# A four-layer graph network on one core: the due times of its planned instruction order are set anew

## The chip, the cores and the metric

The kernel runs on one core of a Trainium2 chip. The core has five engines that matter here: TensorE (PE; matmuls, with PEld for its weight loads), VectorE (DVE), ScalarE (ACT), GpSimd (POOL) and SyncE (SP), which issues all the kernel's DMAs from one queue. The metric is the device time of one execution in microseconds (us); the time before is the median of three runs.

## The reference

128 graphs of 64 nodes carry 512 features in float32. Four layers follow each other, each on a normalized and rectified copy of x, and each added to x:

```python
for each layer: h = max(layernorm(x), 0); x = x + layer(h, adj)
layer 0: relu(conv(h, W1)), layernorm with gamma and beta, conv(., W2), + h
         conv(h, W) = Dn * H @ (Be * H^T @ (h @ W^T)) + b,   H = (adj != 0)
layer 1: s = (h @ w) @ a;  A = exp(leaky(8 tanh((s_i + s_j) / 8))) * adj, rows normalized
         and scaled by the row sums of adj;  A @ h @ w
layer 2: exp(q k^T) * adj, rows normalized, @ v   with q, k, v = h @ Wq, Wk, Wv + biases
layer 3: transition = rows of adj * exp(leaky(s_i + s_j + ab)), normalized
         relu(sum over k = 0..2 of transition^k @ h @ Wk[k] + bk[k])
```

## The kernel before

The rows (128 graphs x 64 nodes) are cut into 16 groups of four tiles of 128 rows, two graphs to a tile. Layers 0 and 1 run over all 16 groups first, with W1, W2 and w resident; x after layer 1 goes to DRAM (xm). Then layers 2 and 3 run over the 16 groups, in the same memory with other tiles: the product Wq^T Wk (made at the start, L477, kept in DRAM as wg_d) and Wv take W1's place (wa_mem), and layer 3's weights are streamed for every group from seven prepared factors in DRAM (fac), which GpSimd works out beside layers 0 and 1 (setup_w3).

All the larger products are in a form with seven block products in place of eight: `strassen` (L691, layers 0 and 1), `prod` in layer2 (L930, called lq for the logits' side and v for the values) and `product` in layer3 (L1124, both by blocks and nested, so 7 x 7 small products of three 128x128 matmuls for k). VectorE makes the sums and differences of the operands (L683, L916, L1091, L1104), ScalarE and VectorE take the results out of PSUM. Transposes go through ScalarE (L601, L603) and a transposing DMA (L602). Layer 3's weights land in three buffers wf (L1116), two loads for each of the seven products, 768 and 576 KB; in the last group two other buffers serve as well. PSUM has eight buffers (ps), shared by everything.

The order of the work is not the order of the code. Each operation is recorded with an engine, an estimated cost and a due time (`Graph.op`); `Graph.run` then plays the whole program once with these costs, before anything is emitted, and emits the instructions in the order that results. At each step it looks, for every engine, at the operations whose inputs are ready and whose buffers are free, takes those that can start soonest, and among them the one with the smallest due time. Each engine then works through its own list strictly in that order on the chip. Where the plan leaves TensorE idle for more than 1 us and a PSUM buffer is free, `fill` puts matmuls on a tile of ones (L1199), so many that half the foreseen gap is filled.

A due time is `G.prio + G.shift`. `G.prio` begins at the group's number times PERIOD1 (layers 0 and 1) or, behind 16 times PERIOD1, times PERIOD2 (layers 2 and 3), and grows within a layer by the cost of each TensorE step times that layer's STRETCH. `G.shift` is the offset from the table AT that `part(name)` sets for the part of the program being recorded: g0 to g3 and g (the product Wq^T Wk and its way to DRAM), bq (a bias from Wk), x0, w1, w2, w (first loads), l0, l1, l3 (preparations), c1, c2, c (sums of weight blocks), wg (load and sums of layer 2's weights), m to y1 (layer 0), s to e1 (layer 1), hT to pv (layer 2), s3 to b0 (layer 3), ws (layer 3's weight loads), load1 to load3. beg0 and beg1 are added to `G.prio` for the first group, end00, end01 and end11 in layers 0 and 1 of the last two groups, new2 and new3 for the first, end2 and end3 for the last group of layers 2 and 3.

```python
pick = min(((t, o) for t, o in can if t <= by), key=lambda c: (c[1].prio, c[1].seq))
```

Of the kernel before, what the change touches and what calls it, by code (L numbers as in the profile page):

```python
# [171 lines left out]
def tile_adj_preln_d4(  # L172
# [40 lines left out]
    def size(shape):  # L213
        n = 1
        for d in shape[1:]:
            n *= d
        return n

    for two in TWO:
        both = work.tile([P, max(sum(size(shape) * n for _, shape, n in tags) for tags in two)], F32,  # L220
                         name="_".join(tag for tags in two for tag, _, _ in tags))
        for tags in two:
            at = 0
            for tag, shape, n in tags:
                for i in range(n):
                    v = both[:, at:at + size(shape)]
                    at += size(shape)
                    if len(shape) == 3:
                        v = v.rearrange("p (a b) -> p a b", a=shape[1])
                    elif len(shape) == 4:  # L230
                        v = v.rearrange("p (a b c) -> p a b c", a=shape[1], b=shape[2])
# [52 lines left out]
    def quad(b):  # L284
# [2 lines left out]
    FILL, LAT = 0.5, 2.3  # L287


    STRETCH, PERIOD1, PERIOD2 = (2.4612, 8.078, 75.6572, 3.3564), 83.325, 154.352  # L290
    AT = {
        "x0": -994.6, "apart": -498.0, "w1": 324.19, "b1": 226.55, "w2": 2150.56, "w": 142.04, "c1": -38.37, "l0":
        -925.08, "c2": 112.02, "l1": -0.36, "c": -1301.28, "g0": -738.7, "g1": -448.93, "g2": -273.36, "g3":
        -517.97, "g": -716.27, "bq": -558.39, "l3": -245.42, "wg": -1135.2, "wp": 1053.37, "beg0": -576.12, "beg1":
        -46.39, "end00": 344.71, "end01": 1612.85, "end11": 614.38, "new2": -75.28, "new3": -60.89, "end2": -113.22,
        "end3": -536.67, "load1": -428.24, "load2": 720.79, "m": -35.26, "h0": -17.03, "p0": 19.05, "z0": -475.95,
        "q0": 27.48, "y0": -539.17, "h1": -22.94, "p1": -22.85, "z1": -30.23, "q1": 5.26, "y1": -136.9, "s":
        -548.75, "t0": -653.3, "e0": -587.74, "t1": -339.5, "e1": -183.15, "hT": 477.73, "sh": -540.0, "lq": 571.58,
        "pt": 1630.65, "v": -264.99, "pv": 1213.51, "s3": 1112.96, "tt": 524.31, "a0": 1110.99, "b0": -1096.16,
        "a1": 1142.82, "ws": 1188.92, "load3": -885.85, "bk": 940.93,  # L300
    }

    def part(name):
# [997 lines left out]
def _program(arrays, n_tokens):  # L1301
    import concourse.bacc as bacc

    nc = bacc.Bacc("TRN2", target_bir_lowering=False, num_devices=1)
    args = [nc.dram_tensor(f"in_{k}_dram", arrays[f"in_{k}_dram"].shape, F32, kind="ExternalInput").ap()
            for k in _NAMES]
    args.append(nc.dram_tensor("out_0_dram", (n_tokens, D), F32, kind="ExternalOutput").ap())
    with tile.TileContext(nc) as tc:
        tile_adj_preln_d4(tc, *args)
    return nc  # L1310
# [12 lines left out]
```

## Time and profile before

| | us |
|---|---|
| median of 3 runs (2337.66 to 2342.29) | 2342.09 |
| the profiled execution, its own time | 2345.87 |
| its span, first to last instruction | 2344.1 |
| TensorE busy | 2292.1 |
| VectorE busy | 1859.1 |
| ScalarE busy | 1388.6 |
| GpSimd busy | 1201.2 |

The profile gives times in us unless marked ns. "Busy" is the union of an engine's instructions; 14280 matmuls are among the 39830 instructions. In answers by windows the columns are: the window, its length, the busy time and count of PE, PEld, DVE, ACT and POOL, then the granted TensorE clock (1 is full), the busy share of the 16 DMA engines, and GB/s. Lists in order of time give start, length, engine, line, operation, output and inputs, and in brackets the idle time before and what ended it. L691 is line 691 of the kernel.

The 16 DMA engines are busy a third of the time in layers 0 and 1 and nearly four fifths in layers 2 and 3, where they move some 220 GB/s. The kernel moves 355 MB in all.

### The profile page before, as it was taken

The page shows a single profiled execution, that of the slowest core. Times are in us where ns is not written, and L with a number is a line of the kernel's source. Part 1 is how long each engine was busy: PE and PEld are TensorE (multiplying, and loading weights), DVE is VectorE, ACT ScalarE, POOL GpSimd, SP SyncE. Part 2 cuts the span into 40 slices and gives each one's busy share as a digit, 9 for nine tenths or more (in the row PEclk, how much of TensorE's full clock was granted, in tenths as well). Part 3 has the DMA queues.
Part 4 walks back from the last instruction along what each step waited for, and adds up shares of the span by engine and source line. Part 5 has one row for each costly group of instructions (what it writes and reads, how often), then busy time and mean ns, then how long its engine had stood idle before and what let it go on. Part 6 is the DMA issues. An engine that isn't in the chain of part 4 may idle for free.

```text
span 2344.1 us, 39830 instructions
## 1 busy us (share of the span) xinstructions
PE 2292.1 (98%) x14280; PEld 1873.0 (80%) x14280; DVE 1859.1 (79%) x4004; ACT 1388.6 (59%) x1993; POOL 1201.2 (51%) x1771
## 2 busy tenths in 40 slices
PE   8999999999999999999999999999999999999997
PEld 4576677776777767777688899999899999999997
DVE  7887887887878777777857778878788888788886
ACT  4666565575555666556746566556566656656642
POOL 7345556545565455554323455445555545555533
PEclk9999999999999999999999999999999999999999
DMA  7343333333333432323415877777787787797757
GB/s 247 85 99 88 78 91 80 96 91 79 79 89 94 96 74 67 78 64 81 106 57 148 237 215 231 216 225 216 219 229 224 222 222 220 211 245 226 224 180 229
DMA packets 403478, 355.12 MB, mean 151 GB/s; under 512 B 290896, under 2 KB 321872, under 8 KB 403280
## 3 DMA queue, kind: packets, MB, share of 16 engines
q1 hardware_dynamic: 403280, 352.58, 54.8%
q8 instruction: 112, 1.84, 0.3%
q14 instruction: 86, 0.70, 0.1%
HBM read 241.05 MB, written 44.33 MB: 122 GB/s over the span
## 4 chain that ended last, share of the span: by engine, by line
PE 79%; DMA 6%; DVE 4%; ACT 3%; issue 1%; POOL 1%; SPq 0%; DVEq 0%; ACTq 0%; POOLq 0%
PE ps L691 34%; PE ps L1124 18%; PE ps L930 15%; PE ps L592 4%; DMA w2m_wm_a_wf<-fac 3%; PE ps L844 2%; PE ps L1067 2%; PE ps L999 2%; PE ps L961 1%; DMA adj<-in_adj_dram 1%; DMA rw<-row 1%; ACT h L583 1%; DMA h<-o 1%; ACT o L601 1%; DVE st L562 1%
## 5 line engine op out<-in xcount | busy, mean ns | idle before, releaser
L583 ACT ACTIVATE h<-x,nm,rs 128x512 f32<-128x512 f32 x384 | 308.6, 816 | 251.3 <-POOL nm L570 233.9
L564 POOL TENSOR_SCALAR rs<-mv 128x1 f32<-128x1 f32 x320 | 118.3, 371 | 388.0 <-DVE mv L563 362.1
L1124 PE MATMUL ps<-w2m_wm_a_wf 128*128 128x128 f32 x2256 | 295.7, 276 | 5.1 <-DMA w2m_wm_a_wf<-fac 4.5
L1124 PEld LDWEIGHTS ps<-w2m_wm_a_wf 128*128 128x128 f32 x2256 | 277.1, 193 | 10.3 <-issue 2.9
L691 PE MATMUL ps<-w2m_wm_a_wf,s_s_zz 128*128 128x256 f32 x1152 | 276.9, 379 | 4.5 <-DVE s_s_zz L683 4.0
L1124 PE MATMUL ps<-w2m_wm_a_wf,tmp_mB_xi 128*128 128x128 f32 x1968 | 259.0, 277 | 10.1 <-DMA w2m_wm_a_wf<-fac 6.6
L691 PEld LDWEIGHTS ps<-w2m_wm_a_wf,s_s_zz 128*128 128x128 f32 x1152 | 217.1, 190 | 52.4 <-issue 18.9
L1124 PEld LDWEIGHTS ps<-w2m_wm_a_wf,tmp_mB_xi 128*128 128x128 f32 x1968 | 239.4, 193 | 15.3 <-issue 4.9
L691 PE MATMUL ps<-w2m_wm_a_wf,rT_vu_tt 128*128 128x256 f32 x1024 | 240.0, 381 | 4.1 <-ACT u L659 2.4
L691 PE MATMUL ps<-wa_mem,mT_sx 128*128 128x512 f32 x512 | 239.1, 593 | 0.8 <-DMA wa_mem<-in_W1T_dram 0.5
L691 PEld LDWEIGHTS ps<-w2m_wm_a_wf,rT_vu_tt 128*128 128x128 f32 x1024 | 193.7, 191 | 42.9 <-issue 11.3
L565 POOL TENSOR_TENSOR rs<-rs,mhalf 128x1 f32<-128x1 f32 x320 | 208.6, 652 | 25.3
L562 DVE BATCH_NORM_STATS2 st<-x 128x6 f32<-128x512 f32 x256 | 175.4, 685 | 15.3 <-DMA x<-xm 7.7
L691 PE MATMUL ps<-wa_mem,s_s_zz 128*128 128x512 f32 x384 | 181.1, 595 | 1.4 <-DVE z_hT L711 1.4
L691 PEld LDWEIGHTS ps<-wa_mem,mT_sx 128*128 128x128 f32 x512 | 96.0, 190 | 106.5 <-issue 98.8
L570 POOL TENSOR_SCALAR nm<-mv,rs 128x1 f32<-128x1 f32 x320 | 159.3, 498 | 31.2
L603 ACT COPY rT_vu_tt<-z_hT 128x1024 uint16<-128x1024 uint16 x128 | 146.6, 1159 | 18.1 <-DMA z_hT<-tmp_mB_xi 17.9
L601 ACT COPY o<-h 128x1024 uint16<-128x1024 uint16 x128 | 134.0, 1048 | 32.5 <-DVE h L1056 29.5
L592 PEld LDWEIGHTS ps<-bd,h 128*128 128x128 f32 x1024 | 127.4, 192 | 25.7 <-DVE bd L873 10.5
L831 ACT ACTIVATE z_hT<-z_hT,nm,rs 128x512 f32<-128x512 f32 x128 | 103.6, 811 | 66.7 <-POOL nm L570 66.5
L982 POOL TENSOR_TENSOR u<-u,wp_bv_bk 128x512 f32<-128x512 f32 x48 | 61.4, 1280 | 155.9 <-ACT u L634 155.9
L601 ACT COPY tmp_mB_xi<-z_hT 128x1024 uint16<-128x1024 uint16 x128 | 133.7, 1045 | 9.3 <-issue 3.0
(205 smaller groups left out, 4975.8 us busy)
## 6 DMA issues: line engine op xcount, KB each, us to landing
w2m_wm_a_wf<-fac SPq DMA_DIRECT2D x110, 768.0 KB, 5.2
w2m_wm_a_wf<-fac SPq DMA_DIRECT2D x109, 576.0 KB, 4.8
x<-xm SPq DMA_DIRECT2D x128, 256.0 KB, 3.8
x<-in_x_dram SPq DMA_DIRECT2D x64, 256.0 KB, 2.8
xm<-x SPq DMA_DIRECT2D x64, 256.0 KB, 2.0
out_dram<-x SPq DMA_DIRECT2D x64, 256.0 KB, 3.7
adj<-in_adj_dram SPq DMA_DIRECT2D x32, 256.0 KB, 3.4
fac<-wp_bv_bk SPq DMA_DIRECT2D x63, 128.0 KB, 2.0
```

Of the source, the lines that this page charges most:

```text
L562: dve(0.69, lambda i=i: nc.vector.bn_stats(st.t[:, i, :], src(i)), [r[i]], [(st, i)])
L564: small(0.28, lambda: nc.gpsimd.tensor_scalar_add(rs.t, mv.t[:, 1:2], EPS), [mv], [rs])
L565: small(0.62, lambda: nc.gpsimd.tensor_tensor(rs.t, rs.t, mhalf, ALU.pow), [rs], [rs])
L570: small(0.32, lambda: nc.gpsimd.tensor_scalar(nm.t, mv.t[:, 0:1], rs.t, -1.0, op0=ALU.mult, op1=ALU.mult), [mv, rs], [nm])
L583: act(0.82, lambda: nc.scalar.activation(h.t, xx.t, AF.Relu, bias=nm.t, scale=rs.t), [xx, nm, rs], [h])
L592: nc.tensor.matmul(quad(p)[:, c, :], h.t[:, c * P:(c + 1) * P], rhs(), start=True, stop=True)
L601: act(1.05, lambda: nc.scalar.copy(u16(planes.t).rearrange("p (q c) -> p q c", q=2), u16(src()).rearrange("p (c q) -> p q c", q=2)), ksrc, ...
L603: act(1.16, lambda: nc.scalar.copy(u16(dst()).rearrange("p c (k q) -> p c k q", q=2), u16(back()).rearrange("p (q c r) -> p c r q", q=2, c ...
L691: nc.tensor.matmul(p.t[:, :n], lhs()[:, c, :], rhs(c), start=first and c == 0, stop=c == kc - 1, skip_group_check=True)
L831: act(0.72, lambda half=half, rs=rs, nm=nm: nc.scalar.activation(half(), half(), AF.Identity, bias=nm.t, scale=rs.t), [(z, j), rs, nm], [( ...
L930: nc.tensor.matmul(pair(p.t)[:, o, :], a, b, start=first and o == 0 and c == 0, stop=c == 1, skip_group_check=True)
L1124: nc.tensor.matmul(inner(p, q)[:, r, :], at()[:, k, :], wv()[:, r, k, :], start=first and r == 0 and k == 0, stop=k == 2, skip_group_check ...
```

## The change

Only numbers change: the four stretches, the two periods and the 61 offsets of AT. No operation, cost, buffer or dependency is touched. The new numbers come from a choice that judges an order by its planned time and by two replays of it, with transfers landing later and with work taking longer.

```diff
-    STRETCH, PERIOD1, PERIOD2 = (2.4612, 8.078, 75.6572, 3.3564), 83.325, 154.352
+    STRETCH, PERIOD1, PERIOD2 = (2.4948, 23.7591, 14.6346, 4.8494), 85.831, 149.366
     AT = {
-        "x0": -994.6, "apart": -498.0, "w1": 324.19, "b1": 226.55, "w2": 2150.56, "w": 142.04, "c1": -38.37, "l0":
-        -925.08, "c2": 112.02, "l1": -0.36, "c": -1301.28, "g0": -738.7, "g1": -448.93, "g2": -273.36, "g3":
-        -517.97, "g": -716.27, "bq": -558.39, "l3": -245.42, "wg": -1135.2, "wp": 1053.37, "beg0": -576.12, "beg1":
-        -46.39, "end00": 344.71, "end01": 1612.85, "end11": 614.38, "new2": -75.28, "new3": -60.89, "end2": -113.22,
-        "end3": -536.67, "load1": -428.24, "load2": 720.79, "m": -35.26, "h0": -17.03, "p0": 19.05, "z0": -475.95,
-        "q0": 27.48, "y0": -539.17, "h1": -22.94, "p1": -22.85, "z1": -30.23, "q1": 5.26, "y1": -136.9, "s":
-        -548.75, "t0": -653.3, "e0": -587.74, "t1": -339.5, "e1": -183.15, "hT": 477.73, "sh": -540.0, "lq": 571.58,
-        "pt": 1630.65, "v": -264.99, "pv": 1213.51, "s3": 1112.96, "tt": 524.31, "a0": 1110.99, "b0": -1096.16,
-        "a1": 1142.82, "ws": 1188.92, "load3": -885.85, "bk": 940.93,
+        "x0": -4068.55, "apart": 224.07, "w1": 516.04, "b1": 32.66, "w2": 1532.85, "w": 425.78, "c1": 13.98, "l0":
+        149.95, "c2": 136.14, "l1": 1002.12, "c": -1662.02, "g0": -2814.3, "g1": -3952.99, "g2": -1010.53, "g3":
+        -2050.55, "g": 1240.85, "bq": -428.92, "l3": 6.32, "wg": 972.96, "wp": 802.66, "beg0": -1575.78, "beg1":
+        40.63, "end00": 26.13, "end01": -76.47, "end11": 345.59, "new2": -84.41, "new3": 49.74, "end2": -49.26,
+        "end3": -79.88, "load1": -66.6, "load2": 1145.31, "m": -45.36, "h0": 0.61, "p0": 28.1, "z0": -564.7, "q0":
+        43.44, "y0": -935.79, "h1": -17.17, "p1": -0.73, "z1": -197.26, "q1": 19.6, "y1": -10.73, "s": -339.5, "t0":
+        -551.91, "e0": -2068.74, "t1": -437.68, "e1": -307.59, "hT": 577.79, "sh": 701.24, "lq": 750.06, "pt":
+        68.58, "v": 596.9, "pv": 1346.35, "s3": 855.54, "tt": 848.03, "a0": 873.02, "b0": 546.14, "a1": 1000.99,
+        "ws": 2292.43, "load3": -1042.83, "bk": 70.08,
     }
```

## The prediction

> **What bounds the kernel now.** I read the totals first, then the stages, then TensorE's own instructions in order of time at the places where the stages lose.
>
> Of the page, the busy times:
> ```profile
> PE 2292.1 (98%) x14280; PEld 1873.0 (80%) x14280; DVE 1859.1 (79%) x4004; ACT 1388.6 (59%) x1993; POOL 1201.2 (51%) x1771
> ```
> Of the busy time by stage (start, layers 0 and 1, the change-over to layers 2 and 3, those two, the end):
> ```profile
> 0.00:140.00 140.00, 125.65 (x465) 75.77 (x466) 112.44 (x227) 81.57 (x117) 71.88 (x101) 0.96 0.54 152
> 140.00:1140.00 1000.00, 995.31 (x4322) 715.97 (x4321) 800.08 (x1755) 613.58 (x855) 546.92 (x861) 1.00 0.34 83
> 1140.00:1310.00 170.00, 159.70 (x1014) 139.66 (x1013) 119.31 (x267) 102.25 (x146) 61.45 (x105) 0.99 0.50 129
> 1310.00:2245.00 935.00, 925.60 (x7690) 859.48 (x7690) 751.64 (x1615) 560.09 (x827) 484.31 (x657) 1.00 0.78 223
> 2245.00:2344.00 99.00, 85.88 (x796) 82.12 (x795) 75.58 (x144) 31.13 (x50) 36.64 (x48) 0.98 0.63 206
> ```
> TensorE bounds everything: it idles 14.4, 4.7, 10.3, 9.4 and 13.1 us in the five stages, 52 in all. Busy time flatters it, since the end of a matmul overlaps the next. In unbroken runs a matmul of 512 columns starts every 0.430 us (four in 1.72), of 256 every 0.216, of 128 every 0.1115 (twelve in 1.33), a half-height one of L1067 every 0.059. By the groups' counts that is 1064 x 0.430 + 4736 x 0.216 + 5728 x 0.1115 + 1024 x 0.059 and 54 for the small forms (0.03 to 0.04 each): 2233 us of useful work. 180 filling matmuls (L1199) on ones add 20. So the span of 2344.1 holds about 90 us that TensorE waits or runs slowly, and 20 of filling: 110 that an order could touch, against 52 by the busy row. [...]
>
> By steady periods: a group of layers 2 and 3 returns every 68.8 us (a pair of matmul runs at 1405.75 and ten groups later at 2093.45) and holds 112 x 0.216 + 294 x 0.1115 + 16 x 0.22 + 64 x 0.059 + 2.6 = 66.9 us of matmuls: 1.9 lost, 30 in 16 groups. A group of layers 0 and 1 returns every 72.2 (370.65, four later 659.57) and holds 71.5: 0.7 lost, 11 in all. The rest, some 50, and all fillings lie at the start, the change-over and the end.
>
> The start, TensorE in order of time (start, length, instruction; in brackets the idle time and its releaser):
> ```profile
> 8.64 5.37 PE L477 MATMUL ps<-tmp_mB_xi 128*128 128x512 f32 x8 [3.82 <-DMA tmp_mB_xi<-in_Wk_dram]
> ...
> 22.62 5.21 PE L477 MATMUL ps<-tmp_mB_xi 128*128 128x512 f32 x8 [1.59 <-DMA tmp_mB_xi<-in_Wk_dram]
> ...
> 32.10 1.95 PE L691 MATMUL ps<-wa_mem,mT_sx 128*128 128x512 f32 x4 [0.54 <-DMA wa_mem<-in_W1T_dram]
> 33.89 2.74 PE L477 MATMUL ps<-tmp_mB_xi 128*128 128x512 f32 x6
> ```
> Until W1 lands at 32 us TensorE has only the Wq-Wk product (L477) to do, and does half of it; the other 16 matmuls follow after 33.89 between layer 0's.
>
> The change-over:
> ```profile
> 1141.69 2.17 PE L1199 MATMUL ps<-ones 128*128 128x128 f32 x18
> 1145.29 1.99 PE L691 MATMUL ps<-w2m_wm_a_wf,s_s_zz 128*128 128x256 f32 x8 [1.43 <-DVE s_s_zz L683]
> ...
> 1160.91 3.29 PE L1199 MATMUL ps<-ones 128*128 128x128 f32 x28
> 1166.75 1.99 PE L691 MATMUL ps<-w2m_wm_a_wf,s_s_zz 128*128 128x256 f32 x8 [2.55 <-DVE s_s_zz L683]
> ```
> These are two holes in layer 0 of the last group, 4.0 us of idling and 46 fillings (5.1): nothing else was let on. Up to 1301 come 1.23, 1.51, 2.30 and smaller waits (6.3) and 38 fillings (4.2).
>
> Layers 2 and 3, TensorE's waits for one transfer in 1320 to 2220 (total, times, longest) and the longest place:
> ```profile
> PE ps L1124 <- DMA w2m_wm_a_wf<-fac: 6.7, 11, 2.1
> ```
> ```profile
> 1667.13 2.54 PE L1124 MATMUL ps<-w2m_wm_a_wf,tmp_mB_xi 128*128 128x128 f32 x12 [2.08 <-DMA w2m_wm_a_wf<-fac]
> ```
> Layer 3's weights come late at times. After such a hole the clock falls: 1660 to 1670 shows 0.88, and the stretches of 60 us from 0, 60, 1260 and 1620 show 0.94, 0.97, 0.97, 0.97: 3.6 + 1.8 x 3 = 9 us lost to the clock, some 1.7 for each drop. [...]
>
> **The change, part by part.** No operation is added or removed; only the number of fillings may move, each 0.11 us in a hole that the order foresees. What changes is the due time of each operation, by which an engine chooses among those that can start soonest. Due times follow from the code (sum of steps times stretch, plus offset); the order that they give I only argue.
>
> *Start.* Before, the Wq-Wk loads and products are due at -739, -449, -273, -518 for the four parts, mixed with group 0's layer 0 (-576) and the Wk loads for the bias (-558). After: -2814, -3953, -1011, -2051, ahead of nearly all of group 0 (about -1576; the bias at -429). Two parts are loaded at once and the others as their buffers come free. Against this, part 1 is issued before part 0, which the sum over parts needs first: by SP's 0.45 us an issue, part 0 goes out 0.8 us later than now (3.06). If all 32 matmuls are through when W1 lands, 16 x 0.43 = 6.9 us no longer lie after it. Not all is kept: between 75 and 101 us TensorE already waits 5.6 (1.65, 2.36, 0.99, 0.59) for ScalarE and VectorE, and it would be there sooner. W1's own load falls behind much the same transfers in both. I take -5, between -7 and +4 (the late part, a further drop of the clock and one more wait).
>
> *Change-over.* Before, layer 1 of group 14 is due at 2920, behind layer 2 of group 0 (1736 and later): it is kept as cover for 1189 to 1237. After, it is due at 1268, ahead of layer 0 of group 15 (1314). Its matmuls, 32 x 0.1115 + 56 x 0.216 = 15.7 us, can fill the two holes worth 9.1. What was cover is then missing later; and the loads and VectorE steps that make layer 2's weights move from due 198, first, to 2346, last (ten steps, 8 x 0.69 + 2 x 0.42 = 6.4 us; VectorE has 30% to spare here). If their SP issues and these steps slip, layer 2 of group 0 starts late, with layer 1 of group 15 as the only cover. I give 4 back: -5, between -10 (the holes and nothing back) and +12 (6.4 us of steps late, a hole of 2 to 4 and a drop of the clock).
>
> *Layers 0 and 1.* Stretch and period hardly move for layer 0, and it loses 0.7 a group: 0, by ±5.
>
> *Layers 2 and 3.* The classes stay in order: before, hT 478, lq 602 to 1386, v 952 to 1736, layer 3's products 1328 to 1422, then pt, pv, s3, a0 from 2848 on; after, hT 578, lq 756 to 907, v 832 to 984, products 1040 to 1176, tt and s3 1313, a0 1348, pv 1759. Only pt goes to the front (305), which frees its PSUM bank sooner. A period further the next group's lq lies at 905 to 1056 and its v at 981 to 1133, in steps of 25 beside the products' 23; before, all seven products fell into one step of 131 of lq. So the runs should alternate more finely, which gives the weights longer to land. But the trace alternates already, since three weight buffers force it (L930 x8 at 1581.58 and 1588.66, L1124 between). I take 0, between -12 (all waits for weights go, 6.7, and three drops of the clock) and +30 (each group loses 1.9 once more).
>
> *End.* s3 of the last group comes behind the products of group 14 in both, and the last products are fed by transfers in both: 0, by ±8.
>
> Sum: -5 - 5 = -10 from the profiled execution's 2345.87, or 2335.9; that execution lay 3.8 above the median of 2342.09, so 2332 as a median.
>
> **Rivals.**
> *A, the edges gain, the steady part stands: 2332.* For it speak the holes that have work due now. Chance 0.40.
> *B, slower: PSUM in layers 2 and 3.* With three streams due alike, lq holds 3 banks, v 3, layer 3's two chains 4: ten of eight, and the step that starts a0 needs four at once, pv two. A stream left open longer makes that step late, then the products, and TensorE has a hole. The order knows the eight banks, and TensorE seldom waits here now; but it plans without the chip's late transfers. At 1.9 us more a group it is +30 - 10 = 2362; at 1.4 us, 2355. It decides from 0.6 us a group, where the edges' gain is used up; above 0.9 it is slower by over 0.2%. I take 2355. Chance 0.38.
> *C, due times only break ties and the buffers set the order: within 0.2%, 2342.* 98% busy speaks for it, the large shifts at the edges against. Chance 0.14.
> *D, the waits for weights go too: -10 - 10 = 2322.* Chance 0.08.
>
> About 0.2% (4.7 us) is what a measurement can tell from no change. Faster: A and D, 0.48; same: C, 0.14; slower: B, 0.38. The range, from D with some of the end (2316) to B's full price (2362), takes in all but some 2 in 10. A's own is 2322 to 2338.
>
> **What would show it.** Start: all L477 before the first L691, and TensorE's idle time up to 140 below 12. Change-over: no wait for L683 near 1145 and 1166, fewer than 84 fillings there, L930 still beginning by about 1175. Layers 2 and 3: a period of 68.8 (A), above 69.4 (B), below 68.3 (D), and the wait for weights near 6.7. I am wrong if the loss moves into the middle, or if layer 2's weights, now last, open a hole.

## The result

The changed kernel takes 2325.17 us, the median of four runs (2320.07 to 2326.38), against 2340.86 for the one before (2337.66 to 2342.29): a ratio of 0.9931, 95% interval 0.9911 to 0.9950. Run once more beside other experiments it had 0.9911 (0.9894 to 0.9929). So it is faster by 0.7 to 0.9%, 16 to 20 us. The profiled execution took 2324.02 us, its span 2322.2, which is 21.9 less than the profiled execution before.

The page after, busy times:
```profile
PE 2281.3 (98%) x14282; PEld 1867.9 (80%) x14282; DVE 1842.0 (79%) x4004; ACT 1393.0 (60%) x1993; POOL 1196.3 (52%) x1771
```
The number of fillings went from 180 to 182, and all else is the same work. Equal windows of time hold different work in the two traces, so I cut the second one where as many us of useful matmuls, by the rates of the prediction, had been started as in the first at 140, 1140, 1310 and 2245. The same five stages of the changed kernel:
```profile
0.00:132.40 132.40, 122.03 (x462) 74.54 (x463) 108.22 (x219) 80.75 (x113) 71.39 (x102) 1.00 0.54 159
132.40:1135.20 1002.80, 998.51 (x4351) 719.66 (x4351) 798.75 (x1764) 616.18 (x860) 549.99 (x860) 1.00 0.34 83
1135.20:1292.90 157.70, 153.86 (x985) 134.45 (x984) 117.27 (x259) 100.48 (x144) 56.91 (x101) 1.00 0.53 140
1292.90:2225.20 932.30, 922.02 (x7692) 857.13 (x7690) 744.17 (x1621) 563.99 (x827) 480.95 (x662) 1.00 0.78 223
2225.20:2322.20 97.00, 84.88 (x799) 82.13 (x798) 73.58 (x144) 31.63 (x50) 37.05 (x48) 0.98 0.65 218
```
The second number is the length of the stage. The gain lies in the first and the third. The clock reads 1.00 in all but the last, but that column counts the drops from full clock alone: from 10.5 to 13.6 us it reads 1.00 too, and there the first four of the 16 matmuls from 10.52 below start, 0.85 us or more apart, where the last twelve start every 0.43. So in this execution the clock came up only at 13.6 us, and the 16 take 8.65 us, where 16 x 0.430 are 6.9. In a table, with other profiled executions that the text comes to (us of each stage; the cut falls at the matmul that reaches the amount, so before has 140.3 and so on):

| | start | layers 0, 1 | change-over | layers 2, 3 | end | span |
|---|---|---|---|---|---|---|
| before | 140.3 | 1000.5 | 169.4 | 935.0 | 98.9 | 2344.1 |
| changed | 132.4 | 1002.8 | 157.7 | 932.3 | 97.0 | 2322.2 |
| changed, again | 131.9 | 1005.3 | 157.2 | 933.9 | 96.5 | 2324.8 |
| a_start | 158.1 | 1004.4 | 158.1 | 937.0 | 97.1 | 2354.7 |
| a_l23 | 131.7 | 1002.4 | 167.8 | 942.6 | 98.6 | 2343.1 |
| a_wg | 131.6 | 1009.9 | 161.9 | 1000.1 | 108.2 | 2411.7 |
| b_end01 | 142.4 | 1002.5 | 166.0 | 944.0 | 98.2 | 2353.1 |
| b_change | 142.8 | 1001.7 | 174.4 | 944.3 | 97.9 | 2361.1 |
| b_wg | 142.0 | 1003.9 | 170.5 | 934.3 | 98.8 | 2349.5 |
| b_late | 140.4 | 1003.8 | 169.2 | 976.3 | 100.3 | 2390.0 |
| a_late | 133.6 | 1002.6 | 158.9 | 967.3 | 98.7 | 2361.1 |

The start after, TensorE in order of time:
```profile
10.52 8.65 PE L477 MATMUL ps<-tmp_mB_xi 128*128 128x512 f32 x16 [1.66 <-DMA tmp_mB_xi<-in_Wk_dram]
...
24.68 5.42 PE L477 MATMUL ps<-tmp_mB_xi 128*128 128x512 f32 x12 [1.33 <-DMA tmp_mB_xi<-in_Wk_dram]
30.10 7.48 PE L691 MATMUL ps<-wa_mem,mT_sx 128*128 128x512 f32 x16
```
Two parts of the Wq-Wk product now run in one piece, 28 of its 32 matmuls lie ahead of layer 0's first product (16 before), and that one begins at 30.10 in place of 32.10, without a wait.

The change-over after, where the two holes were:
```profile
1136.11 1.05 PE L1199 MATMUL ps<-ones 128*128 128x128 f32 x8
1137.95 1.99 PE L691 MATMUL ps<-w2m_wm_a_wf,rT_vu_tt 128*128 128x256 f32 x8 [0.79 <-ACT rT_vu_tt L603]
1139.78 1.50 PE L1199 MATMUL ps<-ones 128*128 128x128 f32 x12
1141.93 1.99 PE L691 MATMUL ps<-w2m_wm_a_wf,s_s_zz 128*128 128x256 f32 x8 [0.65 <-DVE s_s_zz L683]
```
They are 20 fillings and 1.44 us of idling, where there were 46 and 3.98. Behind them layer 1 of group 14 runs from 1150 on (L592 and L691 on mT), beside layer 0 of group 15.

### The profile page after: what moved, and what is told of

Same layout as the page of the kernel before. It is cut to its first block, busy times and chain, and to the rows that moved or that the text cites. A ratio compares the mean times of both kernels' runs of the same rounds, so it can differ in the third digit from the quotient of the medians.

```text
span 2322.2 us, 39841 instructions
## 1 busy us (share of the span) xinstructions
PE 2281.3 (98%) x14282; PEld 1867.9 (80%) x14282; DVE 1842.0 (79%) x4004; ACT 1393.0 (60%) x1993; POOL 1196.3 (52%) x1771
## 4 chain that ended last, share of the span: by engine, by line
PE 82%; DMA 7%; DVE 4%; ACT 3%; issue 2%; POOL 1%; SPq 1%; DVEq 0%; ACTq 0%; POOLq 0%
PE ps L691 38%; PE ps L1124 18%; PE ps L930 14%; PE ps L592 4%; DMA w2m_wm_a_wf<-fac 2%; PE ps L844 2%; DMA x<-xm 2%; PE ps L1067 1%; PE ps L999 1%; PE ps L961 1%; DMA wa_q<-o 1%; ACT h L583 1%; DVE st L562 0%; DMA z_hT<-tmp_mB_xi 0%; DMA tmp_mB_xi<-in_Wk_dram 0%
## 5 line engine op out<-in xcount | busy, mean ns | idle before, releaser
L564 POOL TENSOR_SCALAR rs<-mv 128x1 f32<-128x1 f32 x320 | 105.1, 329 | 383.2 <-DVE mv L563 361.5
L691 PE MATMUL ps<-w2m_wm_a_wf,s_s_zz 128*128 128x256 f32 x1152 | 274.8, 379 | 2.5 <-DVE s_s_zz L683 2.3
L691 PEld LDWEIGHTS ps<-w2m_wm_a_wf,s_s_zz 128*128 128x128 f32 x1152 | 217.3, 190 | 41.0 <-issue 8.9
L691 PE MATMUL ps<-wa_mem,mT_sx 128*128 128x512 f32 x512 | 240.0, 593 | 1.7 <-ACT u L659 1.6
L691 PE MATMUL ps<-w2m_wm_a_wf,rT_vu_tt 128*128 128x256 f32 x1024 | 237.9, 379 | 1.4 <-ACT rT_vu_tt L603 0.8
L691 PEld LDWEIGHTS ps<-w2m_wm_a_wf,rT_vu_tt 128*128 128x128 f32 x1024 | 193.2, 190 | 47.4 <-issue 18.2
L570 POOL TENSOR_SCALAR nm<-mv,rs 128x1 f32<-128x1 f32 x320 | 172.8, 541 | 30.2
L691 PE MATMUL ps<-wa_mem,s_s_zz 128*128 128x512 f32 x384 | 180.1, 593 | 0.2 <-DVE s_s_zz L683 0.2
L691 PEld LDWEIGHTS ps<-wa_mem,mT_sx 128*128 128x128 f32 x512 | 95.0, 190 | 98.5 <-issue 91.4
L818 ACT ACTIVATE z_hT<-z_hT 128x512 f32<-128x512 f32 x128 | 79.4, 630 | 140.1 <-DVE z_hT L711 140.1
L592 PEld LDWEIGHTS ps<-bd,h 128*128 128x128 f32 x1024 | 126.4, 192 | 37.7 <-issue 26.9
L719 POOL TENSOR_TENSOR u<-u,row_sh 128x256 f32<-128x256 f32 x96 | 74.3, 783 | 157.2 <-DVE u L661 136.2
L885 POOL TENSOR_TENSOR x<-x,u 128x256 f32<-128x256 f32 x96 | 87.9, 941 | 118.1 <-DVE u L663 114.1
```

Source lines behind the costliest of these rows:

```text
L564: small(0.28, lambda: nc.gpsimd.tensor_scalar_add(rs.t, mv.t[:, 1:2], EPS), [mv], [rs])
L570: small(0.32, lambda: nc.gpsimd.tensor_scalar(nm.t, mv.t[:, 0:1], rs.t, -1.0, op0=ALU.mult, op1=ALU.mult), [mv, rs], [nm])
L592: nc.tensor.matmul(quad(p)[:, c, :], h.t[:, c * P:(c + 1) * P], rhs(), start=True, stop=True)
L691: nc.tensor.matmul(p.t[:, :n], lhs()[:, c, :], rhs(c), start=first and c == 0, stop=c == kc - 1, skip_group_check=True)
L885: pool(0.78, lambda: nc.gpsimd.tensor_add(xx.t[:, cols], xx.t[:, cols], U.t[:, iu]), [xx, u], [xx])
```

## The experiments

Two theories were set against each other. *E, edges*: each stage's new order has its own gain, and the gains add. *W, whole*: the numbers hang together, and a part of them alone gives something else. A third, *K*, put the gain down to the clock: the execution before had five drops of it ahead of the end, the changed one none from 13.6 us on, where its clock came up. All ratios are to the kernel before, run beside them. The names beginning with a_ are the changed kernel with something set back, those with b_ the kernel before with something new.

**a_start: the start set back.** Twenty offsets, of which the ones that bear on the Wq-Wk product are
```diff
-  "g0": -2814.3, "g1": -3952.99, "g2": -1010.53, "g3": -2050.55, "g": 1240.85, "bq": -428.92, "beg0": -1575.78
+  "g0": -738.7, "g1": -448.93, "g2": -273.36, "g3": -517.97, "g": -716.27, "bq": -558.39, "beg0": -576.12
```


> The changed kernel with the 20 offsets of the start (x0 to l3, beg0, beg1) set back to their old values; change-over, layers 2 and 3 and the stretches keep the new ones. Theory E (edges: each stage's order has its own gain, and they add): the start loses again what it had gained, about 6 us by the time that 100 us of useful matmuls are done, TensorE's idle time up to 140 us goes from 10.4 back to about 14 and the clock falls again there two or three times; the change-over keeps its gain. Time 2331, ratio to the kernel before about 0.9955. Rival K (clock: most of the gain is that the five drops of the clock, 1.7 us each, no longer happen): only the drops of the start come back, 3 x 1.7 = 5, much the same time, but idle time up to 140 would stay near 10. Rival W (whole: the order hangs together and parts do not add): the later stages move too, by 5 us or more at equal useful work.

Measured: 2361.98, ratio 1.0074 (1.0049 to 1.0100): slower than the kernel before, and 31 us above E's 2331. The table shows where: 25.7 us in the start alone, and every later stage within 5 us of the changed kernel. TensorE idles 22.8 us in this start and 88 fillings lie in it, against 10.4 and 30 in the changed kernel, so it is not the clock alone, as K had it. TensorE's waits in a_start up to 157.9 us (total, times, longest):
```profile
PE ps L691 <- DVE s_s_zz L683: 6.1, 3, 3.8
PE ps L477 <- DMA tmp_mB_xi<-in_Wk_dram: 4.4, 2, 4.2
PE ps L592 <- ACT bd L793: 3.4, 2, 2.9
PE ps L691 <- ACT rT_vu_tt L603: 2.9, 1, 2.9
```
The old wait for Wk is back, and new ones of layer 0 behind it. So the loss stays in its stage, as E says, but its size does not fit E: the numbers of the start belong to those of layers 0 and 1, and the old start with the new layers is 18 us worse than with the old ones. No run changes the four g offsets alone, so the share of the early Wq-Wk product by itself is not shown.

**b_end01 and b_change: the change-over alone.**
```diff
-  "end00": 344.71, "end01": 1612.85, "end11": 614.38, "wg": -1135.2, "new2": -75.28, "new3": -60.89, "bk": 940.93
+  "end00": 26.13, "end01": -76.47, "end11": 345.59, "wg": 972.96, "new2": -84.41, "new3": 49.74, "bk": 70.08
```
b_end01 has only the second of these.

> The kernel before with one number new: end01, the offset of layer 1 of group 14, from 1612.85 to -76.47. Theory E with the cover of the two holes as cause: the holes at 1145 and 1166 (4.0 us idle, 46 fillings, 9.1 together) go, and what was cover is missing after 1189, so at most 9 us faster and perhaps nothing, 2332 to 2341; I say 2336, ratio 0.998. If the gain of the change-over (11.6 us at equal useful work) needs the other offsets too, 2341 with the holes gone from 1145 and new ones of like size at 1190 to 1250. Rival K: no change but for drops of the clock.

> The kernel before with the seven offsets of the change-over new (end00, end01, end11, wg, new2, new3, bk). Theory E: it gains by itself what the changed kernel gained there, 9 to 12 us: 2330, ratio 0.9955, with fewer than 10 us of idle time and fillings between 1130 and 1250. Rival W: the seven numbers were chosen with the others, and alone they give less than 4 us or a loss.

Measured: b_end01 2357.29, ratio 1.0043 (1.0029 to 1.0057); b_change 2361.49, ratio 1.0063 (1.0046 to 1.0079). Both lose. b_end01 does shorten the change-over, by 3.4 us, and then loses 9 in layers 2 and 3; b_change lengthens it by 5 and loses 9 as well. In layers 2 and 3 they have 46 and 36 fillings, where the kernel before has none: there, too, holes open while these layers fill up. The expectation of a gain from the cover alone fell; W held for b_change.

**a_l23: layers 2 and 3 set back.**
```diff
-  STRETCH = (2.4948, 23.7591, 14.6346, 4.8494), PERIOD2 = 149.366
+  STRETCH = (2.4948, 23.7591, 75.6572, 3.3564), PERIOD2 = 154.352
```
and the offsets load2, hT to load3, ws, end2 and end3.

> The changed kernel with stretch, period and offsets of layers 2 and 3 set back (load2, hT to load3, ws, end2, end3). Theory E: start and layers 0 and 1 as in the changed kernel; the steady part loses its 4.6 us at equal useful work (among them one drop of the clock), the change-over partly its gain since load2 and hT belong to it: 2330 to 2337, I say 2333, ratio 0.9965. If the finer alternation of layers 2 and 3 mattered more than its 4.6 us show, 2340 or more. Rival W: the change-over falls apart, 2345 or more.

Measured: 2346.92, ratio 1.0007 (0.9991 to 1.0022), as W had it. The whole gain is gone, though start and layers 0 and 1 are those of the changed kernel. It is lost while layers 2 and 3 fill up: change-over and what follows are 20 us longer. Its largest holes there:
```profile
1230.58 3.96 PE L1199 MATMUL ps<-ones 128*128 128x128 f32 x34
1237.74 5.41 PE L930 MATMUL ps<-z_hT,wa_mem 128*128 128x256 f32 x16 [3.20 <-ACT z_hT L603]
...
1324.43 3.74 PE L1199 MATMUL ps<-ones 128*128 128x128 f32 x32
1331.54 3.78 PE L930 MATMUL ps<-wa_mem,row_sh 128*128 128x256 f32 x8 [3.38 <-DVE row_sh L916]
```
Layer 2 of the second and third group is not ready when layer 2 of the one before is through. Later the old numbers are as good as the new: from 1300 to 2160 us of useful work a_l23 needs 879.6 us, the changed kernel 879.9. If the two layers alternate more finely there, it is worth nothing that shows.

**b_wg and a_wg: the weights of layer 2 last or first.**
```diff
-  "wg": -1135.2      (b_wg: new; a_wg: the other way round)
+  "wg": 972.96
```


> The kernel before with one number new: wg from -1135.2 to 972.96, so that the load and sums of layer 2's weights come last instead of first. The prediction gave 4 us for them being late. Theory E: VectorE and SP have room, they are done as soon as they can be either way: within 3 us of before, ratio 0.999 to 1.001, the steady period of layers 2 and 3 unchanged. Rival W, after one number in the other direction cost the changed kernel 91 us: another cycle in layers 2 and 3, 20 us or more.

> The changed kernel with one number old: wg, the offset of the load and the VectorE steps of layer 2's weights, from 972.96 back to -1135.2, so first again in place of last. The prediction feared that last was too late and gave 4 us for it. Theory E: first instead of last costs nothing or gains up to 4 us at the change-over, and layers 2 and 3 keep their period of 68.7: 2321 to 2328. Rival W (the order is one whole; the steady part is a cycle that the change-over leads into, and there is more than one): the order of all of layers 2 and 3 settles differently, though none of their numbers changed; the order that the due times give here foresees a period about a tenth longer, so 2325 + 15 x 6.9, about 2430.

Measured: b_wg 2349.34, ratio 1.0004 (0.9991 to 1.0017): in the kernel before, last costs nothing, as E had it. a_wg 2416.00, ratio 1.0282 (1.0234 to 1.0330): first, in the changed kernel, costs some 85 us, of which 68 lie in layers 2 and 3, whose own numbers are untouched. The 14 periods from the first to the fifteenth m2 step (L1046, the square of a group's transition matrix) of those layers take 74.0 us each on average (1275.4 to 2310.8) against 68.6 (1262.1 to 2223.0). In this stage TensorE idles 38.1 us in place of 10.3 and starts 176 fillings (20 us) in place of none, and drops of the clock take up to 12 us more (it reads 0.99 in place of 1.00). One of the places, TensorE of a_wg:
```profile
1488.55 3.63 PE L999 MATMUL ps<-rT_vu_tt,bd 128*128 128x257 f32 x16
1495.66 1.12 PE L1046 MATMUL ps<-rT_vu_tt,bd 128*64 128x64 f32 x16 [3.48 <-DVE x L1005]
```
and VectorE there:
```profile
1489.36 0.41 DVE L1022 TENSOR_TENSOR ee<-ee,adj 128x256 f32<-128x256 f32 x1
...
1491.58 2.51 DVE L1036 STREAM_TRANSPOSE rT_vu_tt<-bd 32x128 f32<-32x128 f32 x8
...
1495.12 0.88 DVE L1005 SCALAR_TENSOR_TENSOR x<-ps,ve,x 128x256 f32<-128x256 f32 x2
```
A group's transition matrix for layer 3 is made on VectorE only after the next group's values (L930) are through, and that group's attention (L999) runs ahead of m2. Its eight outputs fill all eight PSUM buffers, and m2 needs one too. The transposes end at 1494.09, but m2 starts at 1495.66 only: the wait ends with VectorE's reading of the attention out of PSUM (L1005). Of TensorE's waits in this stage the one of m2 for L1005 is the largest in total, 11.9 us in five. In the changed kernel the same transposes have ended by 1604.04, while the values still run, and m2 follows ahead of the attention, without a wait for it:
```profile
1602.79 1.25 DVE L1036 STREAM_TRANSPOSE rT_vu_tt<-bd 32x128 f32<-32x128 f32 x4
```
```profile
1605.82 0.69 PE L1046 MATMUL ps<-rT_vu_tt,bd 128*64 128x64 f32 x16
1606.43 1.14 PE L999 MATMUL ps<-rT_vu_tt,bd 128*128 128x257 f32 x4
```
The loop of layers 2 and 3 thus has more than one way to run, and in the changed kernel one due time outside it decided which. For a_wg the forecast of W held (2430 foreseen); for b_wg, the same number in the kernel before, it did not.

**a_fill0 and b_fill0: no fillings.**
```diff
-    FILL, LAT = 0.5, 2.3
+    FILL, LAT = 0.0, 2.3
```


> The changed kernel without its 182 filling matmuls (FILL 0.0); the order of all other instructions is the same. It computes the same. Rival K (the clock makes the gain): the holes that the fillings shorten become holes of 2 us and more, about eight of them, and the clock falls behind most, 1.7 us each: 2325 + 8 to 13, about 2335, granted clock 0.994 or below. Theory E: the holes stay holes, what follows them waits for the other engines anyway, and a drop there costs little: within 4 us of the changed kernel, 2321 to 2329.

> The kernel before without its 180 fillings, all other instructions in the same order. Rival K: more drops of the clock (holes at 1, 1141, 1161, 1249, 2249 and 2303 grow past 2 us), 5 to 10 us slower, ratio 1.003. Theory E: within 4 us, ratio 0.9985 to 1.0015.

Measured: a_fill0 2329.92, ratio 0.9915 (0.9886 to 0.9944), within the interval of the changed kernel itself; b_fill0 2353.56, ratio 1.0018 (1.0001 to 1.0036), between what E and K had foreseen. a_fill0 had four drops of the clock ahead of the end (granted clock 0.997), and takes as long as the changed kernel does, as far as an interval of 7 us to each side tells. The clocks of the other executions say more: with a mean granted clock of 0.999 the kernel before took 2343.06 us (one execution) and the changed one, run beside it, 2322.91 to 2330.91 (three). K is out as the main cause.

**after_again: the changed kernel once more.**

> The changed kernel again, beside the others of this series on one chip. Expected: ratio to the kernel before 0.993, and in the profile the same split by equal useful work as the first time: start 6 to 8 us shorter than before, change-over 10 to 12, the rest within 3. Rival K (clock): where the profiled execution has two or more drops of the clock, it should be 3 us or more longer than the first one, which had none before its end.

Measured: 2327.62, ratio 0.9911. The split is much the same: start 8.4 and change-over 12.2 us shorter than before, both a little more than expected, and layers 0 and 1 4.8 longer, where 3 was the bound. This profiled execution had two drops and is 2.6 us longer than the first, less than K asked. They lie at 7.9 and 147.8 us; the start with the one is 0.5 us shorter than in the first execution, layers 0 and 1 with the other 2.5 longer. The five drops before (at 8.7, 22.3, 80.3, 1302.3 and 1667.5 us) last 3.41 us each, at a granted clock of 0.50, and so can cost 1.7 each at most, 8.5 of the 21.9 us between the profiled executions; what they do cost is not shown, and it may be less: b_late, which differs from before in its later stages alone, lacks the drop at 80 us, and its start is as long (140.4 and 140.3).

**b_late and a_late: later weights.** Ahead of each load of layer 3's weights goes a copy from DRAM to DRAM, on the same queue:
```diff
+    nc.sync.dma_start(more, fac[f - 1][n][:, :P])
     nc.sync.dma_start(wv(), fac[f - 1][n]...)
```


> The kernel before with a copy of 64 KB from DRAM to DRAM issued ahead of each load of layer 3's weights (224 copies, one queue, no other instruction moved), so that these loads land later. The output is the same. Expected for both kernels: each issue adds some 0.35 us to SP's queue and the weights land 0.4 to 1 us later; TensorE waited 11.9 us for weights here. Theory R (the changed order stands late landings better): before loses 15 to 25 us, the changed one half of that. Rival S (layers 2 and 3 alternate as finely in both and have the same margin): both lose alike within 4 us, 5 to 20 each.

> The changed kernel with the same copies of 64 KB ahead of each load of layer 3's weights. Theory R: it loses 3 us or more less than the kernel before with them, ratio to the kernel before at most 0.998. Rival S: it loses as much as the kernel before does, and stays 13 to 19 us ahead of it.

Measured: b_late 2392.73, ratio 1.0191 (1.0174 to 1.0208); a_late 2369.42, ratio 1.0091 (1.0068 to 1.0115). By medians they lose 44.7 and 41.8 us, about twice what was expected at most, and alike, as S had it. The waits of TensorE from 1290 to 2300, of b_late and then of a_late:
```profile
PE ps L1124 <- DMA w2m_wm_a_wf<-fac: 39.2, 35, 2.4
```
```profile
PE ps L1124 <- DMA w2m_wm_a_wf<-fac: 23.0, 30, 1.9
```
In the two profiled executions a_late waits less, and its layers 2 and 3 grow by 35 us against 41. Whether the changed order stands late landings better stays open; if so, by a few us of 40. The order is untouched by the copies, and the wait on these weights was 8.3 us in the changed kernel from 1320 to 2220: the landing of weights is something that layers 2 and 3 are sensitive to, in both kernels. What the copies take from other transfers is in the price too, and was not measured by itself.

## Why the prediction was right, point by point

The forecast was A: the edges gain, the steady part stands, -10 us. The direction and the places were right; the size was too small. That the measured 2325.17 comes near D's 2322 is luck for D: its cause, the end of the waits for weights, did not come.

*Start, -5 forecast, -7.9 measured* (-8.4 in the second profile). The mechanism is the one named: 28 of the 32 matmuls ahead of layer 0 (I had asked for all), idle time 10.4 up to the cut (below 12, as asked). The product did begin later, at 10.52 in place of 8.64. When layer 0's first product begins, the changed kernel is some 5 us ahead by useful matmuls. I had thought that the waits of 75 to 101 us, 5.6 in all, would take a third back; from 62 to 102 they are 4.0, the longest 1.60. The drops of the clock at 22 and 80 us did not come; the one at 9 has no counterpart, since the clock came up only at 13.6. That the offsets of the product do it alone is not shown.

*Change-over, -5 forecast, -11.7 measured* (-12.2). This is the term that was mis-sized most. The two holes, 9.1 us, fell to 1.44 + 20 x 0.1115 = 3.7. But the 4 us that I gave back were not given: layer 2's weights last cost nothing (b_wg, in the kernel before), and the holes up to 1301, instead of growing for want of cover, fell as well. In all 84 fillings and 10.3 us of idling became 56 and 3.8, which is 28 x 0.1115 + 6.5 = 9.6, and one drop of the clock. Layer 2 did begin late, at 1181.85 and not by 1175, but layer 1 of group 14 filled the time ahead. My reason for this stage, cover moved from one place to another, is half a reason only: moved alone (b_end01) it shortens the stage by 3.4 and costs 9 behind it. The stage needs the numbers of layers 2 and 3 as well (a_l23).

*Layers 0 and 1, 0 forecast, +2.3 measured*: 30 more fillings there, 3.3 us, and idle time 4.3 against 4.7.

*Layers 2 and 3, 0 forecast, -2.7 measured*. One drop of the clock is gone, 1.7 at most; idle time is 10.3 against 9.4, so the rest stays unexplained. A group returns every 68.6 us, the sign of A. TensorE's wait for weights is 8.3 us from 1320 to 2220, against 6.7: D did not happen, and the argument from the steps of 25 against 131 was rightly set at nothing. B did not happen in this order, but its kind is real: a_wg is a neighbour by one number with 68 us lost in this stage. PSUM has a part in it, but not as B had it, by three streams of products and four buffers at once for the step that starts a0: the attention takes all eight buffers, because VectorE's chain to the transition matrix is late against the values and m2 falls behind the attention.

*End, 0 forecast, -1.9 measured.*

Sum: -7.9 + 2.3 - 11.7 - 2.7 - 1.9 = -21.9 in the profiled executions, -15.7 and -20.4 in the medians of the two comparisons.

## What to carry to other kernels

When a list of due times is set anew, read the trace at the places where the pipeline fills, changes over and drains: there the orders differed by up to 26 us (start) and 17 us (change-over), and the two long stages by up to 12, as long as the loop ran the same way. Such numbers are not knobs with effects of their own: of the six partial changes none beat the kernel before, four were slower than it, one of them by 68 us, and two took as long. So judge whole orders, each on the chip, and check first whether the loop's period is the same.

## What the runs showed of the hardware

224 copies of 64 KB from DRAM to DRAM, 1/20 of a product's weights each, cost 42 to 45 us, 0.2 us a copy, in a stage where the DMA engines were busy 0.78 of the time in either kernel without them. In the kernel before, the clock fell to 0.50 for 3.41 us behind holes of TensorE of 2.30 us (up to 1301.43, the fall at 1302.3) and 2.08 us (up to 1667.13, the fall at 1667.5), and did not behind one of 2.55 (up to 1166.75; from 1165.9 to 1172 it reads 1.00). So the length of a hole alone did not tell here where the clock fell.
